# Graph-weighted attention: the next batch's graph products in one block, and the denominators moved by a burst

## The chip, the cores and the metric

The kernel runs on one core of a Trainium2 chip. The metric is device time in microseconds (us) of one launch, as the median of several runs. The core has five engines with queues of their own: TensorE (PE) for matrix products, VectorE (DVE), ScalarE (ACT) and GpSimd (POOL) for elementwise work, and SyncE (SP), which here only starts transfers. An instruction waits in its engine's queue until what it reads is written and what it overwrites has been read; the other engines go on meanwhile.

## The reference

The input x has 16 batches of 1024 nodes with 256 channels, all float32. Layer 0 is attention whose queries come from a graph product; layer 1 is a graph convolution with two batch norms. Cut to what matters here:

```python
c_adj = mean(x, over channels)                       # one number per node
A     = abs(abs(sigmoid(c_adj[m] - c_adj[n]) - 0.5) - 0.5) * 2
Wg    = adj * A                                      # 1024 x 1024 per batch
q     = relu((x.T @ Wg) * para)                      # 256 x 1024: the graph product
k, v  = x @ kv_w
out   = softmax(q k.T * scale) v                     # 4 heads of 64 channels
x     = layernorm(x + out)
x     = layernorm(x + graph_conv(x, adj, W1, b1, ..., W2, b2, ...))
```

The change touches only how the graph product, the softmax denominators and their neighbours of layer 0 are ordered.

## The kernel before

**Attention.** The work of a batch is 32 units: 2 pairs of heads, 2 halves of the queries, 8 chunks of 128 keys. Two units make a burst, so a batch has 16 bursts; `u` counts them from 0 to 15, and the fifth is `u == 4`. For a unit, `scores` (L1043) makes q k.T with four 64x64 matmuls that run side by side into a bank pair of pool "s", and ScalarE takes the exponential into a tile `p` (four buffers). `outputs` (L1059) multiplies `p` with v into two banks `po` of pool "o" (`tile_o`, two buffers), and VectorE adds `p` into `acc` for the denominators; that addition is also the last reader of a `p` buffer. Four bursts make a group (one pair, one half). After its last unit ScalarE copies `po[0]` into `oT`, VectorE adds `po[1]`, transposes the result by squares, and SP stores it; `squares_to_rows` (L1105) loads it back as rows.

**One burst behind.** The loop at L1381 emits the scores of burst j and then the outputs of burst j - 1 (`back(j - 1)`, L1389), so that ScalarE has a burst's time for the exponentials.

**Denominators.** When both halves of a pair are done, `normalise` (L1113) sums `acc` over partitions with matmuls by ones into a bank `den` of pool "t" (`tile_t`, two buffers), ScalarE copies it to `drow`, and small transfers turn it into columns. `residual` (L1138) takes the reciprocal on VectorE and scales and adds the rows into x on GpSimd. `statistics_x1` and `finish_x1` are the layer norm; the latter runs on ScalarE and ends with a GpSimd transfer of x to memory.

**Graph product.** For the next batch, `weights_abs`, `weights_tanh` (ScalarE) and `weights_adj` (VectorE) make eight tiles `wg` of 128x1024. Then 256x1024 queries come from a scheme of Strassen's kind: seven products instead of eight, each four 128x128 by 128x512 multiplications. Its sums of x are `left_first`, `left_third` and `left_last` (L849 to L859) in a tile `S` with two places; its sums of `wg`, in place, are `right(1)` to `right(4)` (L861), four subtractions each. The products share banks:

| product | reads | bank | after it |
|---|---|---|---|
| 1 | x, wg | pga | copied by ScalarE |
| 3 | S, wg | pgd | copied by ScalarE |
| 2 | x, wg | pga, accumulated | multiplied by para, rectified |
| 6 | S, wg after right(2) | pgb | added by VectorE |
| 7 | S, wg after right(3) | pgb, accumulated | added by VectorE |
| 5 | S, wg after right(1) | pgc | added twice, then weighed and rectified |
| 4 | x, wg after right(4) | pgb, accumulated | added, weighed, rectified |

"Accumulated" means that the product adds onto the bank, so VectorE or ScalarE must have read the earlier value first. All four banks are of pool "t".

**Order around the change.** The order on TensorE, ScalarE, VectorE and SP is the program's own (`manual_schedule`, L1310); semaphores follow from the tiles. Work of other kinds is emitted after `back(j - 1)` of a burst:

- u = 0: seven of the eight key and value steps of this batch, the rest of the `wg` work (`side`), the denominators of the last pair of the batch before.
- u = 1 to 3: residual, statistics of the batch before.
- u = 4 (L1419): products 1, 2, 3 with `left_first` and `right(1)`, the eighth step (keys), `finish_x1`.
- u = 5: row gather, then `load_x(b + 2)`; u = 5, 6, 7: `right(2)`, `right(3)`, `right(4)` (`between`, L920).
- u = 8 (L1428): product 6, `begin` of batch b + 2 (channel sums, reads its x), the denominators of pair 0, products 7, 5, 4.
- u = 9 to 15: one item of the next batch's `side` per burst, residual of pair 0 at 11, `transpose_squares` at 12 and 15; row gathers at 9 and 13.

At batch 14 the diagonal and the row sums of `adj`, for layer 1, come in as well.

Of the kernel before, what the change touches and what calls it, by code (L numbers as in the profile page):

```python
# [515 lines left out]
def fast_path(  # L516
# [46 lines left out]
    def tile_t(name):  # L563
        return psum["t"].tile([P, HALF], F32, tag="t", name=name)
# [168 lines left out]
    with (  # L733
# [49 lines left out]
        def prologue(b):  # L783
# [63 lines left out]
            KC = range(NCH // 2)  # L847

            def left_first():  # L849
                s2, s4 = s["S"][:, 0], s["S"][:, 1]  # L850
                nc.vector.tensor_tensor(s2, A21, A22, ALU.add)
                nc.vector.tensor_tensor(s2, s2, A11, ALU.subtract)
                nc.vector.tensor_tensor(s4, A12, s2, ALU.subtract)

            def left_third():
                nc.vector.tensor_tensor(s["S"][:, 1], A11, A21, ALU.subtract)

            def left_last():
                nc.vector.tensor_tensor(s["S"][:, 0], A21, A22, ALU.add)  # L859

            def right(k):  # L861
                for i in KC:
                    dst, one, two = {
                        1: (lo(i, H1), lo(i, H1), lo(i, H0)),
                        2: (hi(i, H1), hi(i, H1), lo(i, H1)),
                        3: (lo(i, H0), hi(i, H1), lo(i, H0)),
                        4: (hi(i, H0), hi(i, H0), hi(i, H1)),
                    }[k]
                    nc.vector.tensor_tensor(dst, one, two, ALU.subtract)
# [18 lines left out]
            def q_at(c, hs):  # L888
                return s["qT"][:, c, hs]
# [8 lines left out]

            pg = {}

            def p1():
                s["qT"] = qkv.tile([P, CC, N], F32, tag="qT", name=f"qT_{b}")
                s["S"] = xsp.tile([P, 2, NCH // 2, P], F32, tag="xS", name=f"S_{b}")
                pg["a"] = tile_t(f"pga_{b}")
                product(1, pg["a"], True)
                nc.scalar.copy(q_at(1, H0), pg["a"])  # L906
                left_first()
                right(1)

            def p3():  # L910
                pg["d"] = tile_t(f"pgd_{b}")
                product(3, pg["d"], True)
                nc.scalar.copy(q_at(0, H1), pg["d"])

            def p2():
                product(2, pg["a"], False)
                nc.vector.tensor_mul(q_at(0, H0), pg["a"], para_s[:, 0, H0])
                rectify(0, H0)

            def between(u):  # L920
                right(u - 3)
                if u == 6:
                    nc.vector.tensor_add(q_at(0, H1), q_at(0, H1), q_at(1, H0))
                if u == 7:
                    left_third()

            def p6():
                pg["b"] = tile_t(f"pgb_{b}")
                product(6, pg["b"], True)
                nc.vector.tensor_add(q_at(0, H1), pg["b"], q_at(0, H1))  # L930
                left_last()

            def p7():
                product(7, pg["b"], False)
                nc.vector.tensor_add(q_at(1, H1), pg["b"], q_at(1, H0))

            def p5():
# [7 lines left out]
            def p4():  # L945
# [81 lines left out]
            if b:  # L1027
                s["graph"] = dict(
                    between=between, p=(None, p1, p2, p3, p4, p5, p6, p7),
                )  # L1030
            return first, steps, side

# [277 lines left out]
        with tc.manual_schedule(  # L1310
# [70 lines left out]
            for j in range(len(bursts)):  # L1381
                b, u = j // PERB, j % PERB
                for i in bursts[j]:
                    scores(i)
                if u == 0:
                    steps, side = next_steps, next_side
                    next_first, next_steps, next_side = [], [], []
                if j:
                    back(j - 1)  # L1389
                if u in (5, 9, 13):  # L1390
                    run(rows_of, 1)
                if u == 5 and b + 2 < B:
                    load_x(b + 2)
                    next_first, next_steps, next_side = prologue(b + 2)
                if b == B - 1:
                    if u == 0:
                        run(sums, 1)
                        run(rows_of, 1)
                    elif u in (2, 13):
                        run(full, 2)  # L1400
                    elif u == 8:
                        run(sums, 1)
                    elif u == 3:
                        late.clear()
                elif u == 0:
                    for i in range(7):
                        if b:
                            run(steps, 1)
                            run(side, (2, 3, 2, 3, 2, 2, 99)[i])
                        if i == 1:  # L1410
                            run(sums, 1)
                            run(rows_of, 1)
                elif u < 4:
                    if u == 1:
                        run(full, 2)
                    else:
                        run(late, 1)
                    run(side, 99)
                elif u == 4:  # L1419
                    p = st[b + 1]["graph"]["p"]  # L1420
                    keys_last = steps[:1] if b else []
                    del steps[: len(keys_last)]
                    p[1]()
                    run(keys_last, 1)
                    run(late, 2)
                    p[2]()
                    p[3]()
                elif u == 8:  # L1428
                    p = st[b + 1]["graph"]["p"]
                    p[6]()  # L1430
                    run(next_first, 1)
                    run(sums, 1)
                    if b == B - 2:
                        adjacency_diagonal()
                        for n in range(6):
                            adjacency_rows(n)
                    p[7]()
                    p[5]()
                    p[4]()
                elif u < 8:  # L1440
                    st[b + 1]["graph"]["between"](u)
                else:
                    if u == 9 and b + 2 < B:
                        load_squares(b + 2, 0)
                    if u == 11:
                        run(full, 2)
# [602 lines left out]
```

## Time and profile before

| | us |
|---|---|
| median of 3 runs (2445.45 to 2446.09) | 2445.65 |
| the profiled execution's own time | 2446.41 |
| span of that execution, first to last instruction | 2444.6 |
| TensorE busy in the span | 2411.5 |
| VectorE busy | 1862.8 |
| ScalarE busy | 1238.3 |
| GpSimd busy | 475.7 |
| matmuls of scores L1051, outputs L1072 | 488.1, 485.3 |

The mean granted TensorE clock is 0.997 of full speed. Attention takes about the first 1560 us. In the profile a row names engine, line, operation and tiles (`po<-p,v`: po is written from p and v), with the count of instructions merged into it; in brackets stand idle time ahead of it and what ended that. Each 128x512 multiplication in float32 counts as two MATMUL rows. Ends of matmuls are modelled and overlap with the next, so that spacing is read from start to start.

### The profile page before, as it was taken

How to read it: one execution, taken by the hardware profiler on the slowest of the kernel's cores; microseconds unless marked ns; L12 is line 12 of the kernel's file. 1: busy time of each engine (PE TensorE's matmuls, PEld its weight loads, DVE VectorE, ACT ScalarE, POOL GpSimd, SP SyncE). 2: the span in 40 equal slices, each digit the busy share in tenths (PEclk: the TensorE clock that was granted, in tenths of full speed). 3: DMA queues.
4: the chain of work that ended last, by engine and by line, in shares of the span. 5: the costliest groups of instructions: out<-in, count | busy, mean ns of one | idle time of the engine just before them, and what ended most of it. 6: DMA issues, size and time to landing. Idle time of an engine off the chain costs nothing.

```text
span 2444.6 us, 32834 instructions
## 1 busy us (share of the span) xinstructions
PE 2411.5 (99%) x12422; PEld 1029.6 (42%) x12422; DVE 1862.8 (76%) x2570; ACT 1238.3 (51%) x1545; POOL 475.7 (19%) x486
## 2 busy tenths in 40 slices
PE   9999999999999999999999999999999999999997
PEld 5343443443434434434334343344444444444455
DVE  5688878878888888788788888956566566478978
ACT  7376675765765756657647667421110111045568
POOL 0021122111311211122112112422122122010026
PEclk9999999999999999999999999999999999999999
DMA  5124232332232332322322327221222222165559
GB/s 164 40 42 85 57 49 70 70 53 68 38 83 54 48 84 56 53 70 56 63 62 44 83 49 97 82 103 70 96 92 78 94 86 86 69 241 172 172 210 343
DMA packets 423175, 221.99 MB, mean 91 GB/s; under 512 B 361568, under 2 KB 394848, under 8 KB 414560
## 3 DMA queue, kind: packets, MB, share of 16 engines
q1 hardware_dynamic: 417648, 168.94, 28.4%
q0 software_dynamic: 4832, 50.34, 4.9%
q8 instruction: 99, 1.62, 0.3%
q14 instruction: 68, 0.56, 0.1%
q10 hardware_dynamic: 528, 0.52, 0.1%
HBM read 136.06 MB, written 83.69 MB: 90 GB/s over the span
## 4 chain that ended last, share of the span: by engine, by line
PE 86%; DVE 9%; ACT 3%; DMA 1%; issue 1%; POOL 0%; POOLq 0%; DVEq 0%
PE ps L1051 18%; PE po L1072 18%; PE pgb L883 7%; PE b_agg L1556 4%; PE pga L883 4%; PE c_agg L1556 4%; PE pk L980 4%; PE b_o L1763 3%; PE pv L993 3%; PE a_agg L1556 2%; PE b_h L1588 2%; PE pgd L883 2%; PE pgc L883 2%; PE a_o L1763 2%; PE c_o L1763 2%; PE c_h L1588 2%
## 5 line engine op out<-in xcount | busy, mean ns | idle before, releaser
L1056 ACT ACTIVATE p<-ps 128x1024 f32<-128x1024 f32 x512 | 497.6, 1021 | 183.7 <-PE ps L1051 130.1
L1082 DVE TENSOR_TENSOR acc<-acc,p 128x1024 f32<-128x1024 f32 x384 | 500.1, 1302 | 54.2 <-ACT p L1056 29.3
L1051 PE MATMUL ps<-qT,kT 64*64 64x512 f32 x4096 | 488.1, 592 | 0.3 <-ACT p L1056 0.3
L1072 PE MATMUL po<-p,v 64*64 64x512 f32 x4096 | 485.3, 589 | 0.0
L1147 POOL TENSOR_TENSOR o<-o,r_all 128x512 f32<-128x512 f32 x62 | 94.8, 1538 | 1090.8 <-DVE r_all L1141 1052.5
L1072 PEld LDWEIGHTS po<-p,v 64*64 64x64 f32 x4096 | 158.2, 133 | 281.3 <-issue 274.3
L1051 PEld LDWEIGHTS ps<-qT,kT 64*64 64x64 f32 x4096 | 151.4, 133 | 286.8 <-issue 249.2
L834 DVE SCALAR_TENSOR_TENSOR wg<-wg,adj_s 128x1024 f32<-128x1024 f32 x128 | 149.4, 1217 | 16.5 <-ACT wg L830 16.5
L825 ACT ACTIVATE wg<-crow,ccol 128x1024 f32<-128x1024 f32 x128 | 146.8, 1147 | 0.5 <-DMA crow<-c 0.5
L830 ACT ACTIVATE wg<-wg 128x1024 f32<-128x1024 f32 x128 | 136.0, 1062 | 0.9
L980 PE MATMUL pk<-xT,kvw_s 128*128 128x512 f32 x256 | 121.8, 598 | 3.1 <-ACT drow L1126 3.1
L993 PE MATMUL pv<-kvw_s,xT 128*128 128x256 f32 x512 | 124.0, 385 | 0.0
L993 PEld LDWEIGHTS pv<-kvw_s,xT 128*128 128x128 f32 x512 | 94.9, 190 | 50.0 <-issue 13.4
L893 ACT ACTIVATE qT<-qT 128x512 f32<-128x512 f32 x60 | 37.3, 629 | 149.8 <-DVE qT L896 145.2
L883 PE MATMUL pgb<-wg,S 128*128 128x512 f32 x240 | 111.0, 605 | 0.0
L883 PE MATMUL pga<-wg,x 128*128 128x512 f32 x240 | 109.6, 599 | 0.7 <-ACT qT L906 0.7
L1556 PE MATMUL a_agg<-ahT,x1l 128*128 128x512 f32 x240 | 108.1, 593 | 0.7 <-ACT agg L1298 0.7
L1148 POOL TENSOR_TENSOR x<-x,o 128x512 f32<-128x512 f32 x62 | 107.8, 1748 | 2.3
L1556 PE MATMUL b_agg<-aT,x1S 128*128 128x512 f32 x240 | 107.9, 592 | 0.0
L654 ACT COPY p_agg<-a_agg 128x512 f32<-128x512 f32 x15 | 8.8, 586 | 183.3 <-PE a_agg L1556 183.3
L690 POOL TENSOR_TENSOR x1S<-x1l 128x512 f32<-128x512 f32 x15 | 19.0, 1264 | 352.3 <-PE c_agg L1556 349.0
L1080 DVE TENSOR_TENSOR acc<-p,p 128x1024 f32<-128x1024 f32 x64 | 77.4, 1209 | 7.5 <-ACT p L1056 7.5
(230 smaller groups left out, 3511.8 us busy)
## 6 DMA issues: line engine op xcount, KB each, us to landing
h<-hw POOLq DMA_DIRECT2D x16, 2048.0 KB, 6.7
hl<-h SPq DMA_DIRECT2D x32, 1024.0 KB
x<-x POOLq DMA_DIRECT2D x16, 1024.0 KB, 4.2
x1l<-x SPq DMA_DIRECT2D x16, 1024.0 KB
xf<-x SPq DMA_DIRECT2D x16, 1024.0 KB
o<-oS SPq DMA_DIRECT2D x62, 256.0 KB
o<-o SPq DMA_DIRECT2D x248, 64.0 KB
x<-in_x_dram SPq DMA_DIRECT2D x15, 1024.0 KB
```

What stands on the lines that cost most here:

```text
L825: nc.scalar.activation(w, s["crow"], AF.Abs, bias=s["ccol"][:, n : n + 1])
L830: nc.scalar.activation(w, w, AF.Tanh, scale=0.5)
L834: nc.vector.scalar_tensor_tensor(w, w, 1.0, adj_s[:, n, :], op0=ALU.subtract, op1=ALU.mult)
L883: nc.tensor.matmul(ps, left, right, start=(start and i == 0), stop=(i == NCH // 2 - 1), skip_group_check=True,)
L980: nc.tensor.matmul(ps, kvw_s[:, c, kc * P : (kc + 1) * P], s["xT"][:, c, hs], start=(c == 0), stop=(c == CC - 1),)
L993: nc.tensor.matmul(pt[:, j * C : (j + 1) * C], s["xT"][:, c, n * P : (n + 1) * P], kvw_s[:, c, C : 2 * C], start=(c == 0), stop=(c == CC - 1),
L1051: nc.tensor.matmul(ps[kh * D : (kh + 1) * D, hd * HALF : (hd + 1) * HALF], kT[r, pr, ks], qT[r, pr, qh * HALF : (qh + 1) * HALF], start=Tr ...
L1056: nc.scalar.activation(p, ps, AF.Exp)
L1072: nc.tensor.matmul(g["po"][kh][hd * D : (hd + 1) * D, :], s["v"][r, m, h * D : (h + 1) * D], p[r, hd * HALF : (hd + 1) * HALF], start=(m = ...
L1082: nc.vector.tensor_add(g["acc"], g["acc"], p)
L1556: nc.tensor.matmul(ps, left, right, start=(start and i == 0), stop=(i == NCH // 2 - 1), skip_group_check=True,)
L1763: nc.tensor.matmul(ps, left, right, start=(start and i == 0), stop=(i == 1), skip_group_check=True,)
```

## The change

The seven products stand in one block at u = 4, in the order 1, 3, 2, then 6, then 7, 5, 4. `pga` and `pgb` come from pool "o" instead of "t". `left_first` is at the end of u = 0; two of the four subtractions of `right(1)` are at u = 1 and the other two behind product 1; `right(2)` to `right(4)` are between the products. The key step stands behind product 6, `finish_x1` and the `adj` sums between product 2 and product 6, and `load_x(b + 2)` ends the block. `begin` moves to u = 5. The denominators of pair 0 move to u = 9, between that burst's scores and the outputs of the burst before (at the last batch they stay at u = 8). The residual of pair 0 moves from u = 11 to 13, the third row gather from 13 to 15, and two `weights_adj` from u = 0 to u = 11 and 13.

```diff
             def left_first():
+                s["S"] = xsp.tile([P, 2, NCH // 2, P], F32, tag="xS", name=f"S_{b}")
...
-            def right(k):
-                for i in KC:
+            def right(k, rows=KC):
+                for i in rows:
...
-            def p1():
+            def first_three():
                 s["qT"] = qkv.tile([P, CC, N], F32, tag="qT", name=f"qT_{b}")
-                s["S"] = xsp.tile([P, 2, NCH // 2, P], F32, tag="xS", name=f"S_{b}")
-                pg["a"] = tile_t(f"pga_{b}")
+                pg["a"] = tile_o(f"pga_{b}")
                 product(1, pg["a"], True)
                 nc.scalar.copy(q_at(1, H0), pg["a"])
-                left_first()
-                right(1)
-
-            def p3():
+                right(1, KC[2:])
                 pg["d"] = tile_t(f"pgd_{b}")
                 product(3, pg["d"], True)
                 nc.scalar.copy(q_at(0, H1), pg["d"])
-
-            def p2():
+                right(2)
                 product(2, pg["a"], False)
                 nc.vector.tensor_mul(q_at(0, H0), pg["a"], para_s[:, 0, H0])
                 rectify(0, H0)
 
-            def between(u):
-                right(u - 3)
-                if u == 6:
-                    nc.vector.tensor_add(q_at(0, H1), q_at(0, H1), q_at(1, H0))
-                if u == 7:
-                    left_third()
-
             def p6():
-                pg["b"] = tile_t(f"pgb_{b}")
+                left_third()
+                right(3)
+                nc.vector.tensor_add(q_at(0, H1), q_at(0, H1), q_at(1, H0))
+                pg["b"] = tile_o(f"pgb_{b}")
                 product(6, pg["b"], True)
                 nc.vector.tensor_add(q_at(0, H1), pg["b"], q_at(0, H1))
                 left_last()
-
-            def p7():
+                right(4)
+
+            def last_three():
                 product(7, pg["b"], False)
                 nc.vector.tensor_add(q_at(1, H1), pg["b"], q_at(1, H0))
...
-                    (a, 0), (t, 0), (a, 1), (t, 1), (a, 2), (t, 2), (a, 3),
-                    (t, 3), (a, 4), (t, 4), (j, 0), (a, 5), (t, 5), (j, 1),
-                    (a, 6), (j, 2), (j, 3), (t, 6), (j, 4), (a, 7), (j, 5),
-                    (t, 7), (j, 6), (j, 7),
+                    (a, 0), (t, 0), (j, 0), (a, 1), (t, 1), (j, 1), (a, 2), (t, 2),
+                    (a, 3), (t, 3), (j, 2), (a, 4), (t, 4), (a, 5), (j, 3), (t, 5),
+                    (j, 4), (a, 6), (t, 6), (j, 5), (a, 7), (t, 7), (j, 6), (j, 7),
...
+                if u == 9 and b < B - 1:
+                    run(sums, 1)
                 if j:
                     back(j - 1)
-                if u in (5, 9, 13):
+                if u in ((5, 9, 13) if b == B - 1 else (5, 9, 15)):
                     run(rows_of, 1)
-                if u == 5 and b + 2 < B:
-                    load_x(b + 2)
-                    next_first, next_steps, next_side = prologue(b + 2)
...
-                            run(side, (2, 3, 2, 3, 2, 2, 99)[i])
+                            run(side, (2, 2, 2, 2, 2, 2, 99)[i])
...
+                    st[b + 1]["graph"]["left"]()
                 elif u == 4:
                     p = st[b + 1]["graph"]["p"]
-                    keys_last = steps[:1] if b else []
-                    del steps[: len(keys_last)]
-                    p[1]()
-                    run(keys_last, 1)
+                    p[0]()
                     run(late, 2)
-                    p[2]()
-                    p[3]()
-                elif u == 8:
-                    p = st[b + 1]["graph"]["p"]
-                    p[6]()
-                    run(next_first, 1)
-                    run(sums, 1)
                     if b == B - 2:
                         adjacency_diagonal()
                         for n in range(6):
                             adjacency_rows(n)
-                    p[7]()
-                    p[5]()
-                    p[4]()
-                elif u < 8:
-                    st[b + 1]["graph"]["between"](u)
-                else:
+                    p[1]()
+                    if b:
+                        run(steps, 1)
+                    p[2]()
+                    if b + 2 < B:
+                        load_x(b + 2)
+                        next_first, next_steps, next_side = prologue(b + 2)
+                elif u < 4:
+                    if u == 1:
+                        run(full, 2)
+                        st[b + 1]["graph"]["right"](1, range(2))
+                    else:
+                        run(late, 1)
+                elif u == 5:
+                    run(next_first, 1)
+                elif u > 8:
...
-                    if u == 11:
-                        run(full, 2)
...
+                    if u == 13:
+                        run(full, 2)
...
-                    run(next_side, 1)
+                    run(next_side, 2 if u in (11, 13) else 1)
```

More of the change, by code (lines that the diff above doesn't have):

```diff
@@ L931, in p6 @@
                 left_last()
-            def p7():
+                right(4)
+            def last_three():
                 product(7, pg["b"], False)
                 nc.vector.tensor_add(q_at(1, H1), pg["b"], q_at(1, H0))
-            def p5():
                 pg["c"] = tile_t(f"pgc_{b}")
@@ L943, in p5 @@
                     weigh(c, H1)
-            def p4():
                 product(4, pg["b"], False)
@@ L1028, in prologue @@
                 s["graph"] = dict(
-                    between=between, p=(None, p1, p2, p3, p4, p5, p6, p7),
+                    left=left_first, right=right, p=(first_three, p6, last_three),
                 )
@@ L1412, in fast_path @@
                             run(rows_of, 1)
-                elif u < 4:
-                    if u == 1:
-                        run(full, 2)
-                    else:
-                        run(late, 1)
-                    run(side, 99)
+                    st[b + 1]["graph"]["left"]()
                 elif u == 4:
                     p = st[b + 1]["graph"]["p"]
-                    keys_last = steps[:1] if b else []
-                    del steps[: len(keys_last)]
-                    p[1]()
-                    run(keys_last, 1)
+                    p[0]()
                     run(late, 2)
-                    p[2]()
-                    p[3]()
-                elif u == 8:
-                    p = st[b + 1]["graph"]["p"]
-                    p[6]()
-                    run(next_first, 1)
-                    run(sums, 1)
                     if b == B - 2:
@@ L1436, in fast_path @@
                             adjacency_rows(n)
-                    p[7]()
-                    p[5]()
-                    p[4]()
-                elif u < 8:
-                    st[b + 1]["graph"]["between"](u)
-                else:
+                    p[1]()
[14 more added lines that the diff above has]
+                elif u > 8:
                     if u == 9 and b + 2 < B:
                         load_squares(b + 2, 0)
-                    if u == 11:
-                        run(full, 2)
                     if u == 12:
```

## The prediction

> **What bounds the kernel now.** I read the page, then who waited for whom on TensorE, then one batch in order of time on each engine. Batch 10 is used below (u is the burst within it, 0 to 15); its pattern repeats every 96.69 us. Page, busy time and chain that ended last:
>
> ```profile
> PE 2411.5 (99%) x12422; PEld 1029.6 (42%) x12422; DVE 1862.8 (76%) x2570; ACT 1238.3 (51%) x1545; POOL 475.7 (19%) x486
> PE 86%; DVE 9%; ACT 3%; DMA 1%; issue 1%; POOL 0%; POOLq 0%; DVEq 0%
> ```
>
> TensorE sets the time. Its waits in the attention part sum to some 4 us after the first load, the most regular 0.22 us per batch for the denominators' copy (pk behind drow). So a change can save only matmul slots or what is lost between them, and any new TensorE wait adds in full. TensorE in order of time, around the blocks at u = 4 (batch 10) and u = 8 (batch 9):
>
> ```profile
> 1043.53 1.90 PE L1051 MATMUL ps<-qT,kT 64*64 64x512 f32 x16
> 1045.24 1.90 PE L1072 MATMUL po<-p,v 64*64 64x512 f32 x16
> 1047.07 3.70 PE L883 MATMUL pga<-wg,x 128*128 128x512 f32 x8
> 1050.61 1.88 PE L980 MATMUL pk<-xT,kvw_s 128*128 128x512 f32 x4
> ...
> 974.66 1.90 PE L1072 MATMUL po<-p,v 64*64 64x512 f32 x16
> 976.49 3.70 PE L883 MATMUL pgb<-wg,S 128*128 128x512 f32 x8
> 980.12 1.07 PE L1120 MATMUL den<-acc,ones 128*32 128x512 f32 x8
> 981.11 3.70 PE L883 MATMUL pgb<-wg,S 128*128 128x512 f32 x8
> 984.65 3.60 PE L883 MATMUL pgc<-wg,S 128*128 128x512 f32 x8
> 988.08 3.60 PE L883 MATMUL pgb<-wg,x 128*128 128x512 f32 x8
> 991.61 1.95 PE L1051 MATMUL ps<-qT,kT 64*64 64x512 f32 x16
> ```
>
> Go by the starts. A burst's scores or outputs take 1.72 us, a product 3.43, a key step 1.72; two products without a change of tile shape stand 3.43 apart (984.65 to 988.08), with one 3.53 to 3.63. At u = 4 the first product follows the outputs without a wait. ScalarE and VectorE meanwhile:
>
> ```profile
> 1041.20 1.94 ACT L1056 ACTIVATE p<-ps 128x1024 f32<-128x1024 f32 x2 [1.50 <-PE ps L1051]
> 1045.18 1.02 ACT L1056 ACTIVATE p<-ps 128x1024 f32<-128x1024 f32 x1 [2.05 <-DVE acc L1082]
> 1046.51 1.02 ACT L1056 ACTIVATE p<-ps 128x1024 f32<-128x1024 f32 x1 [0.30 <-DVE acc L1082]
> 1047.43 0.58 ACT L1089 COPY oT<-po 128x512 f32<-128x512 f32 x1
> ```
> ```profile
> 1034.86 1.22 DVE L834 SCALAR_TENSOR_TENSOR wg<-wg,adj_s 128x1024 f32<-128x1024 f32 x1 [0.92 <-ACT wg L830]
> 1036.00 1.22 DVE L1080 TENSOR_TENSOR acc<-p,p 128x1024 f32<-128x1024 f32 x1
> 1037.13 0.26 DVE L1141 RECIPROCAL r_all<-dcol 128x8 f32<-128x8 f32 x2
> 1037.32 3.21 DVE L1082 TENSOR_TENSOR acc<-acc,p 128x1024 f32<-128x1024 f32 x2
> 1041.69 0.43 DVE L618 BATCH_NORM_STATS2 st_l<-x 128x6 f32<-128x256 f32 x1 [1.16 <-POOL x L1148]
> 1043.83 2.59 DVE L1082 TENSOR_TENSOR acc<-acc,p 128x1024 f32<-128x1024 f32 x2
> 1050.91 0.68 DVE L1090 TENSOR_TENSOR oT<-po,oT 128x512 f32<-128x512 f32 x1
> ```
>
> VectorE lags from u = 1 on: the exponentials of u = 4 wait for its additions to release a p buffer, and behind them in ScalarE's queue stands the copy of po, done at 1048.01, **0.94 us after** the first product began. Now nothing waits for it, as that product writes another bank.
>
> [...] that copy runs only after the second exponential. [...] `o<-o,r_all` took 1.99 us beside VectorE's additions and 1.04 after them.
>
> **The change, part by part.**
>
> *Drains.* At u = 8 the excesses are 0.11 (into the block), 0.20 and 0.13 (into and out of the denominators), 0.11, 0.10 (out) and 0.05 (scores at 991.61, outputs at 993.38: 1.77): 0.70 us. At u = 4: 0.11 + 0.11 + 0.10 + 0.05 = 0.37. One block keeps 0.37. The denominators between scores and outputs still change shape twice, which before doesn't show: at least one 0.10 and the 0.05, at most 0.60 (nearly twice the pair 0.20 + 0.13); I take that pair once, 0.33. Saved 0.70 - 0.33 = **0.37 us** per batch (0.10 to 0.55), 15 batches. The matmuls themselves are unchanged, as are the 0.22 us behind drow: ahead of that copy stand one abs and one tanh, as before.
>
> *pga and pgb take the pool of po.* It has two banks, both held by the group that ends at u = 4; the bank released first is the one read by ScalarE's copy of po[0] (L1089). So product 1 now waits for that copy. The copy can't start before the outputs drain: at batch 0, where ScalarE is idle, it ran 81.03 to 81.62 against the first product at 80.91. The floor is so 81.66 - 80.91 = **0.75 us**, every batch. With the queue of before it is 1048.01 + 0.05 - 1047.07 = 0.99.
>
> *VectorE's work ahead of u = 4.* The three sums of `left_first` (0.65 + 0.69 + 0.69, 2.0 us in sequence: 955.57 to 957.59) move to the end of u = 0, two subtractions of `right(1)` (0.6 each, from four in 2.41) to u = 1. Two `weights_adj` (1.22 each) leave u = 0, but give nothing back: VectorE idles there and its last one waits for the last tanh (0.92 us, above), which TensorE's last value step paces. So the 2.0 us fall after 1036.0. The reciprocals and GpSimd's residual, which the statistics wait for at 1041.69, come 2.0 later; VectorE itself, busy to 1040.53, comes to 1040.53 + 2.0 + 1.2 = 1043.75. Statistics start at 1043.7 to 1044.1, a shift of 2.0 to 2.4, since GpSimd's add is slower beside VectorE. Everything behind keeps it: additions, exponentials of u = 4, copy of po. I take 2.2: copy ends 1050.2, product 1 starts 1050.26 for 1047.07, **3.2 us late** (0.75 to 3.5). Queued behind product 1 is all of TensorE.
>
> *Inside the block.* From product 2's end E: VectorE does the multiply, `left_third`, four subtractions, two adds (0.6 + 0.6 + 2.41 + 0.6 + 0.6, plus 0.3 of signals) = E + 5.1, and product 7 accumulates on the bank that the last add reads. TensorE arrives after product 6 and the key step, 3.43 + 1.72 = E + 5.15: 0.05 lost. At batch 0 there is no key step: 5.1 - 3.43 = 1.7 lost. At batch 14 the eight diagonal operations stand ahead (1464.90 to 1467.53, 2.6 us): 2.6 lost. Product 5 and 4 are ready in time (`left_last` E + 5.7 before E + 8.6; `right(4)` E + 8.1 before E + 12.0).
>
> *Moved at no cost.* `load_x` now precedes u = 5's row gathers in SP's queue and waits for the x1 store: `finish_x1` stands behind the rectify on ScalarE (E = 1050.26 + 3.54 + 2 x 3.43 = 1060.7, rectified by 1062, eight activations in 4.05), ends at 1066, store 4.2 us, load some 4.6 (issued 965.79, DMA quiet after 970.5), so 1075; `begin` reads it after product 4 (E + 15.5), its adds and u = 5's addition (2.7, as after 991.5 before): 1079. If late, VectorE and then TensorE would wait. The gathers behind it are read at u = 13 only. `begin`'s 2.9 us at u = 5 delays additions that release buffers for u = 7; the subtractions that filled u = 5 to 7 are gone. Residual at u = 13 and the third gather at u = 15 feed u = 1 and later. `weights_adj` 0 and 1 at u = 11 and 13 use idle of 1.77 and 1.15 us; without that cover the copy of v, and the denominators behind it at u = 0, would be up to 0.6 late; I take 0.1.
>
> *Sum.* Batches 1 to 13: 3.2 + 0.05 + 0.1 - 0.37 = 2.98, times 13 = 38.7. Batch 0, with VectorE idle early: 0.75 + 1.7 - 0.37 - 0.68 (product 2's wait for the copy of pga, now covered by product 3) = 1.4. Batch 14: 3.2 + 2.6 + 0.1 - 0.37 = 5.5. Together +45.6. The profiled execution took 2446.41 (span 2444.6), 0.76 above the median 2445.65; against the median: **2491 us**.
>
> **Rivals.**
> *Lag absorbed:* VectorE's extra 3.2 us is swallowed before u = 4, and product 1 loses 0.75 to 1.5. For: VectorE idles 1.16 us at 1041. Against: that idle waits for GpSimd, which shifts too. 13 x (1.1 - 0.22) + 1.4 + 3.4 = +16: 2462.
> *More than one wait:* [...] the copy of v comes 0.6 late, or pga gets the other bank and waits for VectorE's add, 3.6 us later still. [...] Against: the pool gives the first released. [...] the other bank: 2540.
> *Not slower:* only drains count. It decides where they give back what product 1's wait takes: the floor of 0.75 needs a saving of 0.75 per batch, and all of u = 8's excess is 0.70. If the denominators change shape for nothing: 15 x (0.75 - 0.70) + 1 = 2447. Against: ScalarE's lag is in the trace.
>
> **Numbers.** Likeliest 0.72 (own range 2478 to 2504), lag absorbed 0.12, more waits 0.12, not slower 0.04. The range 2460 to 2516 leaves out the not slower case and the far end of the waits. Within 0.2% (4.9 us) is about what this kernel's measurement can't tell from no change: faster 0.02, same 0.03, slower 0.95.
>
> **What would show it.** TensorE's waits: pga behind the copy of po (ACT oT), 14 times near 3 us and once near 0.7; pgb behind VectorE's add once near 1.7 and once near 2.6. In time order no change of shape at u = 8, and denominators between scores and outputs at u = 9. Statistics near 2.2 us later against u = 0's end. Wrong if pga begins without a wait, if VectorE's additions at u = 2 aren't later, or if a longer wait stands elsewhere.

## The result, and the profile after

| | before | after |
|---|---|---|
| median, us | 2445.87 (4 runs) | 2560.02 (4 runs, 2559.24 to 2560.34) |
| ratio after to before | | 1.0465 [1.0447, 1.0483] |
| profiled execution, its span, us | 2446.41, 2444.6 | 2559.24, 2557.4 |
| mean granted TensorE clock | 0.997 | 0.992 |

The change makes the kernel 114 us slower; 46 us were forecast, and the time lies outside the range. The page of the kernel after, busy time, the chain that ended last, and three groups:

```profile
PE 2436.0 (95%) x12422; PEld 1029.2 (40%) x12422; DVE 1922.6 (75%) x2570; ACT 1240.5 (49%) x1545; POOL 512.2 (20%) x486
...
PE 65%; DVE 24%; ACT 6%; issue 4%; DMA 0%; SPq 0%; DVEq 0%; POOL 0%; POOLq 0%; ACTq 0%
...
L1070 DVE TENSOR_TENSOR acc<-acc,p 128x1024 f32<-128x1024 f32 x384 | 544.9, 1419 | 30.5 <-ACT p L1044 2.4
...
L884 PE MATMUL pga<-wg,x 128*128 128x512 f32 x240 | 119.6, 645 | 32.4 <-ACT oT L1077 32.4
...
L1136 POOL TENSOR_TENSOR x<-x,o 128x512 f32<-128x512 f32 x62 | 136.3, 2217 | 0.2
```

Instruction counts are those of before, yet three busy times grew: TensorE by 25 us, VectorE by 60, GpSimd by 36. So the same instructions take longer. VectorE's additions have a mean of 1419 ns, where before it was 1302; GpSimd's `x<-x,o` has 2217, before 1748; the product into pga 645, before 599. On the chain, VectorE's share rose from 9% to 24%.

TensorE's waits in the kernel after (what waited, for whom: total us, times, longest), layer 0 alone:

```profile
PE pga L884 <- ACT oT L1077: 32.4, 15, 2.5
PE ps L1039 <- ACT p L1044: 24.6, 43, 1.1
PE den L1108 <- DVE v L987: 15.1, 14, 1.1
PE pv L982 <- DVE xT L819: 11.8, 14, 0.9
PE pxT L811 <- DMA x<-in_x_dram: 5.0, 1, 5.0
PE pgb L884 <- DVE qT L922: 4.3, 2, 2.6
PE po L1060 <- DVE oT L1078: 3.1, 1, 3.1
```

The first row is the forecast wait, with the forecast releaser: 32.4 us in 15 waits. The next three, 51.5 us, stood in no sum of mine. Apart from the first load, these waits sum to 91.3 us; before it was some 4.

TensorE in order of time in the kernel after, batch 10, from the end of u = 15 through the block at u = 0 to product 1:

```profile
1086.74 0.70 PE L982 MATMUL pv<-kvw_s,xT 128*128 128x256 f32 x2
1088.29 1.56 PE L982 MATMUL pv<-kvw_s,xT 128*128 128x256 f32 x6 [0.85 <-DVE xT L819]
1089.69 1.88 PE L969 MATMUL pk<-xT,kvw_s 128*128 128x512 f32 x4
1092.65 1.06 PE L1108 MATMUL den<-acc,ones 128*32 128x512 f32 x8 [1.08 <-DVE v L987]
...
1102.46 1.95 PE L1039 MATMUL ps<-qT,kT 64*64 64x512 f32 x16
...
1109.72 2.00 PE L1039 MATMUL ps<-qT,kT 64*64 64x512 f32 x16 [0.17 <-ACT p L1044]
...
1113.89 1.09 PE L1039 MATMUL ps<-qT,kT 64*64 64x512 f32 x8 [0.45 <-ACT p L1044]
1116.11 1.09 PE L1039 MATMUL ps<-qT,kT 64*64 64x512 f32 x8 [1.12 <-ACT p L1044]
1117.02 1.90 PE L1060 MATMUL po<-p,v 64*64 64x512 f32 x16
1121.16 5.40 PE L884 MATMUL pga<-wg,x 128*128 128x512 f32 x8 [2.25 <-ACT oT L1077]
1126.39 3.60 PE L884 MATMUL pgd<-wg,S 128*128 128x512 f32 x8
```

The reader can account for a batch by starts. Before, product 1 to product 1 took 96.69 us, of which the block at u = 0 13.93 (1019.24 to 1033.17) and from its end to product 1 13.90 (to 1047.07). After, the preceding product 1 stands at 1017.97, so the batch takes 103.19: the block at u = 0 15.72 (1086.74 to 1102.46), from its end to product 1 18.70 (to 1121.16), the rest 68.77 for 68.86. So 1.79 us are lost at u = 0 and 4.80 on the way to product 1. Of these 4.80 about 2.5 are lost ahead of and between the scores of u = 2 to 4, and 2.3 ahead of product 1 itself (4.14 us after the outputs, where 1.83 was usual). In addition this product 1 lasts 5.23 us up to the next start, where 3.54 was usual.

The windows of that stretch (window, us, TensorE busy and instructions, granted clock, DMA share, GB/s) show why:

```profile
1121.00:1122.00 1.00, 0.84 (x2) 1.00 0.00 0
...
1123.00:1124.00 1.00, 1.00 (x2) 0.50 0.00 0
...
1125.00:1126.00 1.00, 1.00 (x3) 0.61 0.00 0
```

TensorE runs at a granted clock of 0.50 for 3.41 us, behind an idle stretch of 2.25; this product 1 so takes 1.69 us more. The attention part has eight such stretches: six behind product 1, and two behind the single waits of 2.6 us (pgb at batch 14) and 3.1 (po at batch 15). Before had none there, and one in layer 1 that has gone. Seven more at 1.7 us make 12 us.

VectorE in the kernel after, around the same two places:

```profile
1078.61 8.47 DVE L1070 TENSOR_TENSOR acc<-acc,p 128x1024 f32<-128x1024 f32 x4
1087.01 1.23 DVE L819 STREAM_TRANSPOSE xT<-xS 128x1024 f32<-128x1024 f32 x1
...
1091.94 0.65 DVE L987 COPY v<-pv 128x512 f32<-128x512 f32 x1
...
1108.65 2.09 DVE L870 TENSOR_TENSOR wg<-wg 128x512 f32<-128x512 f32 x2
1110.66 4.27 DVE L1070 TENSOR_TENSOR acc<-acc,p 128x1024 f32<-128x1024 f32 x2
1114.86 0.41 DVE L618 BATCH_NORM_STATS2 st_l<-x 128x6 f32<-128x256 f32 x1
```

And GpSimd in the kernel after, the residual of pair 0 at u = 13 and that of pair 1 at u = 1:

```profile
1077.62 3.95 POOL L1135 TENSOR_TENSOR o<-o,r_all 128x512 f32<-128x512 f32 x2 [42.81 <-DVE r_all L1129]
1081.54 4.46 POOL L1136 TENSOR_TENSOR x<-x,o 128x512 f32<-128x512 f32 x2
1108.80 2.84 POOL L1135 TENSOR_TENSOR o<-o,r_all 128x512 f32<-128x512 f32 x2 [22.80 <-DVE r_all L1129]
1111.61 4.45 POOL L1136 TENSOR_TENSOR x<-x,o 128x512 f32<-128x512 f32 x2
```

In the kernel before the same four additions at u = 13 to 15 have no GpSimd beside them, and the second half of the residual at u = 1 runs beside the statistics. Its rows on VectorE and on GpSimd:

```profile
1010.02 5.21 DVE L1082 TENSOR_TENSOR acc<-acc,p 128x1024 f32<-128x1024 f32 x4
```
```profile
1041.62 1.04 POOL L1147 TENSOR_TENSOR o<-o,r_all 128x512 f32<-128x512 f32 x1
1042.74 1.27 POOL L1148 TENSOR_TENSOR x<-x,o 128x512 f32<-128x512 f32 x1
```

Four additions alone take 5.21 us; GpSimd's four operations, with only statistics beside them, would take 2 x (1.04 + 1.27) = 4.62. Together the additions take 8.47 us, 3.26 more, and GpSimd's operations 8.41, 3.8 more. So 3.26 of GpSimd's 4.62 us were added to VectorE's time: the two engines worked largely in turn. In what way they hold each other up is not shown; the time lies within the recorded operations, and no table of waits has it. Beside the statistics GpSimd's operations cost nothing that shows: these took 0.43 and 0.39 us, and 0.42 and 0.39 with GpSimd idle. My prediction gave 1.99 and 1.04 us for such an operation beside the additions and after them, but took no sum of times from them.

### The profile page after: what moved, and what is told of

The parts are those of the page before. It is cut to its first block, busy times and chain, and to the rows that moved or that the text cites. A ratio compares the mean times of both kernels' runs of the same rounds, so it can differ in the third digit from the quotient of the medians.

```text
span 2557.4 us, 32804 instructions
## 1 busy us (share of the span) xinstructions
PE 2436.0 (95%) x12422; PEld 1029.2 (40%) x12422; DVE 1922.6 (75%) x2570; ACT 1240.5 (49%) x1545; POOL 512.2 (20%) x486
## 4 chain that ended last, share of the span: by engine, by line
PE 65%; DVE 24%; ACT 6%; issue 4%; DMA 0%; SPq 0%; DVEq 0%; POOL 0%; POOLq 0%; ACTq 0%
PE po L1060 10%; PE ps L1039 10%; DVE acc L1070 8%; PE pgb L884 6%; PE pga L884 5%; PE b_agg L1538 4%; PE c_agg L1538 4%; PE b_o L1745 3%; PE pk L969 2%; PE a_agg L1538 2%; PE b_h L1570 2%; PE pgc L884 2%; PE pgd L884 2%; PE c_o L1745 2%; PE a_o L1745 2%
## 5 line engine op out<-in xcount | busy, mean ns | idle before, releaser
L1070 DVE TENSOR_TENSOR acc<-acc,p 128x1024 f32<-128x1024 f32 x384 | 544.9, 1419 | 30.5 <-ACT p L1044 2.4
L1039 PE MATMUL ps<-qT,kT 64*64 64x512 f32 x4096 | 497.1, 595 | 24.6 <-ACT p L1044 24.6
L1060 PE MATMUL po<-p,v 64*64 64x512 f32 x4096 | 490.5, 590 | 3.1 <-DVE oT L1078 3.1
L1135 POOL TENSOR_TENSOR o<-o,r_all 128x512 f32<-128x512 f32 x62 | 105.2, 1713 | 1013.0 <-DVE r_all L1129 1013.0
L884 PE MATMUL pga<-wg,x 128*128 128x512 f32 x240 | 119.6, 645 | 32.4 <-ACT oT L1077 32.4
L982 PE MATMUL pv<-kvw_s,xT 128*128 128x256 f32 x512 | 128.2, 389 | 11.8 <-DVE xT L819 11.8
L1136 POOL TENSOR_TENSOR x<-x,o 128x512 f32<-128x512 f32 x62 | 136.3, 2217 | 0.2
L1078 DVE TENSOR_TENSOR oT<-po,oT 128x512 f32<-128x512 f32 x64 | 44.0, 688 | 66.2 <-ACT oT L1077 66.1
```

Source lines behind the costliest of these rows:

```text
L884: nc.tensor.matmul(ps, left, right, start=(start and i == 0), stop=(i == NCH // 2 - 1), skip_group_check=True,)
L982: nc.tensor.matmul(pt[:, j * C : (j + 1) * C], s["xT"][:, c, n * P : (n + 1) * P], kvw_s[:, c, C : 2 * C], start=(c == 0), stop=(c == CC - 1),
L1039: nc.tensor.matmul(ps[kh * D : (kh + 1) * D, hd * HALF : (hd + 1) * HALF], kT[r, pr, ks], qT[r, pr, qh * HALF : (qh + 1) * HALF], start=Tr ...
L1060: nc.tensor.matmul(g["po"][kh][hd * D : (hd + 1) * D, :], s["v"][r, m, h * D : (h + 1) * D], p[r, hd * HALF : (hd + 1) * HALF], start=(m = ...
L1070: nc.vector.tensor_add(g["acc"], g["acc"], p)
L1136: nc.gpsimd.tensor_tensor(xs, xs, o, ALU.add)
```

## The experiments

The theory after the traces was that four causes act in series. (1) The lag of VectorE, from the sums of `left_first` and from GpSimd's turns, which makes the scores of u = 3 and 4 wait and product 1 with them. (2) The bank taken over from po. (3) Work moved to u = 11 to 15 that GpSimd's residual meets there, so that the transposed x and the copy of v come late at u = 0. (4) Half clock behind product 1's wait. The rivals: the scores' waits come from the bank wait; only one of the two moves of (3) is the cause; half clock comes from something else than product 1's wait. The first four kernels undo one part each of the kernel after; gains are given against its 2560.02 us.

**The bank given back.**

```diff
-                pg["a"] = tile_o(f"pga_{b}")
+                pg["a"] = tile_t(f"pga_{b}")
```

> The changed kernel with one edit: pga comes from pool "t" again, pgb stays in pool "o". If product 1's wait for the copy of po is a loss of its own, it goes (2.4 us start to start in 14 batches, 0.7 at batch 0) and with it the stretches at half clock (7 more than before, 1.7 us each): about 2514 us. Rival, VectorE's lag is the bound and the bank only the first place where it shows: the 2.4 us come back at product 6, which needs right(2), and the time stays near 2545.

Measured: 2516.37 us, ratio to before 1.0283 [1.0253, 1.0313], so 44 us of the 114 back. The wait of pga is gone, and with it the six half clock stretches behind it; of the attention part's eight the one of batch 14 is left. The stretch behind po at batch 15 has gone too, while layer 1 has one of 6.8 us (2.9 lost) that the kernel after lacks. So 32.4 + 7 x 1.7 - 2.9 = 41 us are accounted for, of 42.3 between the two profiled executions. The waits of the scores (24.6), the denominators (15.1) and the values (11.8) are unchanged, to the digit.

So the scores don't wait because of the bank, and the half clock in those batches follows from product 1's wait: the waits of up to 1.12 us left in place here bring none. The rival, that the time comes back at product 6, is out.

**The three sums of `left_first` back in VectorE's idle time** within u = 0, behind its fourth value step:

```diff
-                    st[b + 1]["graph"]["left"]()
+                        if i == 3:
+                            st[b + 1]["graph"]["left"]()
```

> The changed kernel with left_first emitted after the fourth step of u = 0, where VectorE idles 3.1 us ahead of the third value step's copy, and not at the end of u = 0. If the lag at u = 1 to 4 is VectorE's added work, its 2.05 us leave the path: waits of the scores and of product 1 shrink by 2.05 us per batch, 29 us, and some half-clock stretches go: 2518 to 2531. Rival, the lag comes from VectorE and GpSimd hindering each other at u = 1 and 2: those rows last as long, and the time falls by less than 10 us.

Measured: 2535.85 us, 1.0362 [1.0332, 1.0392], 24 us back. In TensorE's waits of this kernel those of the scores have shrunk from 24.6 to 3.2 us, and that of product 1 has not moved, against the expectation that both would shrink:

```profile
PE pga L884 <- ACT oT L1077: 32.4, 15, 2.5
...
PE ps L1039 <- ACT p L1044: 3.2, 15, 0.3
```

The gain is the 2.05 us by which those sums end later than the last `weights_adj` of u = 0, 14 times: 29 us. Less was measured because half clock follows product 1 in ten batches here, for six, and three stretches more in all take 5 us back. The wait of product 1 doesn't shrink, since TensorE too now arrives 2 us earlier: from the end of the block at u = 0 to product 1 it is 16.65 us for 18.70.

**The residual of pair 0 back at u = 11**, and, apart, **the two `weights_adj` back at u = 0**:

```diff
+                    if u == 11:
+                        run(full, 2)
...
-                    if u == 13:
-                        run(full, 2)
```
```diff
-                            run(side, (2, 2, 2, 2, 2, 2, 99)[i])
+                            run(side, (2, 3, 2, 3, 2, 2, 99)[i])
...
-                    run(next_side, 2 if u in (11, 13) else 1)
+                    run(next_side, 1)
```

> The changed kernel with pair 0's residual at u = 11 again (denominators stay at u = 9). If GpSimd's four operations at u = 13 to 15 are what makes VectorE late at u = 0 (additions of 2.1 us there for 1.3), the waits for xT (0.85) and for the copy of v (1.08) go, 1.8 us in 14 batches: about 2535. If the two weights_adj at u = 11 and 13 are the cause, the time stays within 5 us of 2560.

> The changed kernel with all eight weights_adj at u = 0 again (the list and the counts of before), residual still at u = 13. If the two that moved to u = 11 and 13 (2.3 us of VectorE) cause the lateness at u = 0, its 1.8 us in 14 batches go: about 2535, with no other loss, since VectorE idles at u = 0. If GpSimd at u = 13 to 15 is the cause, the time falls by less than 8 us.

Measured: 2537.77 us, 1.0370 [1.0340, 1.0400], and 2539.06, 1.0375 [1.0345, 1.0406]: 22 and 21 us back, each most of the 14 x 1.79 = 25 lost at u = 0. In both the wait of pv is gone; that of den is gone in the first and 1.5 us in the second. At batch 10 the block at u = 0 takes 14.08 and 13.94 us, for 15.72 in the kernel after. In the first, the wait for the denominators' copy is back (0.37 us a batch); in the second, the profiled execution has a mean granted clock of 0.991 for 0.992, which by these rounded figures takes some 2.5 us back. With the residual at u = 11, VectorE's four additions and the transpose that TensorE waited for read:

```profile
1066.04 5.21 DVE L1070 TENSOR_TENSOR acc<-acc,p 128x1024 f32<-128x1024 f32 x4
1071.16 1.24 DVE L819 STREAM_TRANSPOSE xT<-xS 128x1024 f32<-128x1024 f32 x1
```

The additions take 5.21 us again, for 8.47. The rival of one cause falls, and the transpose shows why. Before it ended 2.85 us ahead of the block at u = 0 (1016.39 for 1019.24). With the residual back at u = 11 it ends 1.91 us ahead (1072.40 for 1074.31), with the `weights_adj` back at u = 0 still 0.65, and with both moved it ends 1.50 us behind the block's start (1088.24 for 1086.74). Its lead covers either load alone, and not both.

The next two do one part alone in the kernel before. **The bank alone**:

```diff
-                pg["a"] = tile_t(f"pga_{b}")
+                pg["a"] = tile_o(f"pga_{b}")
```

> The kernel before with one edit: pga comes from pool "o". The bank alone makes product 1 wait for ScalarE's copy of po, which in the trace of before ends 0.99 us after that product begins (0.75 at batch 0): 14 x 0.99 + 0.75 = 14.6, so about 2460 us, with no stretch at half clock. Rival: if the copy can be overtaken or the bank of po[1] is handed out, 2446 or about 2510.

Measured: 2462.01 us beside 2446.08, 1.0063 [1.0043, 1.0083], +16. TensorE and its waits:

```profile
1055.43 1.90 PE L1072 MATMUL po<-p,v 64*64 64x512 f32 x16
1058.26 1.98 PE L883 MATMUL pga<-wg,x 128*128 128x512 f32 x4 [0.93 <-ACT oT L1089]
```
```profile
PE pga L883 <- ACT oT L1089: 14.0, 15, 1.2
```

Product 1 starts 2.83 us after the outputs, where 1.83 was usual: 1.00 lost, for a forecast of 0.99 from ScalarE's queue. The first bank that was released is the one handed out. The attention part has no stretch at half clock.

**The sums alone**: `left_first` at the end of u = 0 and two subtractions at u = 1, all else as before.

```diff
+                    st[b + 1]["graph"]["left"]()
...
+                        st[b + 1]["graph"]["right"](1, range(2))
```

> The kernel before with left_first at the end of u = 0 and two subtractions of right(1) at u = 1, as in the changed kernel, all else as it was, pga in pool "t". If VectorE's 3.2 us ahead of u = 4 delay the release of p buffers, the scores of u = 3 and 4 wait as in the changed kernel (1.7 us by its waits, 2.4 start to start): about 2479. Rival, lateness at u = 4 hurts only through the bank: 2446 to 2450.

Measured: 2482.01 us, 1.0145 [1.0124, 1.0165], +36. The scores' waits are those of the kernel after:

```profile
PE ps L1050 <- ACT p L1055: 24.6, 43, 1.1
```

So this move alone produces them. The two parts alone cost 16 + 36 = 52; together, product 1's wait more than doubles, 32.4 us for 14.0. Two runs tell what that rise doesn't need: it stays at 32.4 with `left_first` in idle time (above), and at 25.7 without GpSimd's residual (next). Common to both are the two subtractions at u = 1; no run has them alone with the bank, so their share is not shown.

**GpSimd silent.** The kernel after without GpSimd's two operations per residual; it leaves out that attention is added to x. Everything else runs.

```diff
-                nc.gpsimd.tensor_tensor(oh, oh, r, ALU.mult)
-                nc.gpsimd.tensor_tensor(xs, xs, o, ALU.add)
```

> The changed kernel without GpSimd's two operations of the residual (the attention is not added to x, for all pairs but the last of the last batch), reciprocals and transfers kept. If VectorE's and GpSimd's operations with two inputs run one after the other, the additions last 1.3 instead of 2.1 us; the waits for xT and v at u = 0 go (1.8 us), statistics start 2.4 us earlier and so does product 1: 4.2 us in 14 batches and less half clock, 2493 to 2502. If GpSimd matters only as a producer of x, which VectorE never waits for here, the time stays within 8 us of 2560.

Measured: 2491.98 us, 1.0185 [1.0165, 1.0206], 1 us below the expected range: 68 of the 114 us depend on those two lines, though GpSimd is busy for 20% of the span and no wait of TensorE names it. VectorE's additions and TensorE's waits in this kernel:

```profile
L1070 DVE TENSOR_TENSOR acc<-acc,p 128x1024 f32<-128x1024 f32 x384 | 468.1, 1219 | 31.1 <-ACT p L1044 3.0
```
```profile
PE pga L884 <- ACT oT L1077: 25.7, 15, 2.1
...
PE ps L1039 <- ACT p L1044: 2.6, 15, 0.3
```

The additions have 1219 ns each for 1419: 384 x 0.2 = 77 us less. The waits at u = 0 are gone and those of the scores nearly so, while product 1's wait, the bank's own, stays with 25.7. One half clock stretch is left behind product 1, whose wait is 2.08 us there. This run took away GpSimd's work as well as its place in the order, so 68 us is what its meeting with VectorE costs here, half clock included, not what another placing could win over the kernel before.

**What the one block is worth.** The last three keep the block, the denominators at u = 9 and the residual at u = 13. They undo what the runs above found to cost time: pga is in pool "t" again, `left_first` in idle time, all `weights_adj` at u = 0, all of `right(1)` behind product 1. At batch 14 the `adj` sums go behind the whole block (in the code `p[0]` emits products 1, 3 and 2, `p[1]` product 6, `p[2]` products 7, 5 and 4).

```diff
-                pg["a"] = tile_o(f"pga_{b}")
+                pg["a"] = tile_t(f"pga_{b}")
...
-                right(1, KC[2:])
+                right(1)
...
+                        if i == 3:
+                            st[b + 1]["graph"]["left"]()
...
                     p[2]()
+                    if b == B - 2:
+                        adjacency_diagonal()
```

> The changed kernel with pga in pool "t", left_first in VectorE's idle time in the middle of u = 0, right(1) whole behind product 1, all weights_adj at u = 0, and the diagonal and row sums of adj behind the block at batch 14. One block and the moved denominators stay. If the waits found are all that the change costs, what is left is the saved change of tile shape, 0.41 us in 15 batches, less product 7's wait at batch 0 (1.8) and 0.2 elsewhere per batch: 2441 to 2446. Rival, one block has a cost of its own (VectorE's sums can't keep up inside it): above 2455.

Measured: 2459.82 us, 1.0056 [1.0039, 1.0073], 14 above the expected range and in that of the rival, a cost of one block itself. But the regular waits are gone, and a period is 96.60 us for 96.69. The miss lies in single places: at batch 14 the row sums of `adj`, which I had put where ScalarE takes the exponentials (5.7 us), with them one half clock stretch of 6.8 us, in which TensorE stood still for the first half (1.6 us lost), and single waits of 2.1, 1.8 and 1.0 us elsewhere.

```profile
PE ps L1040 <- ACT p L1045: 6.0, 2, 5.7
```

The next version puts those sums ahead of product 7, moves `left_third` and one addition ahead of the multiply that follows product 2 so that product 7 isn't late, and keeps the row gathers and the residual of batch 14 at u = 13 and 11:

```diff
                 right(2)
+                left_third()
+                nc.vector.tensor_add(q_at(0, H1), q_at(0, H1), q_at(1, H0))
                 product(2, pg["a"], False)
...
-                    if u == 13:
+                    if u == (13 if b < B - 2 else 11):
                         run(full, 2)
```

> The merged kernel with left_third and the addition of the two copies ahead of product 2's multiply, the adj sums of batch 14 ahead of product 7, and batch 14's residual and third gather at u = 11 and 13 as before. In the merged kernel a batch takes 96.60 us from product 1 to product 1 for 96.69 before, with 0.2 us lost ahead of product 7; the rest of its 14 us are single waits at batches 0 (1.8), 14 and 15 (5.7, 2.1, 1.0) and 3.4 us of half-clock loss. Without them: 15 x 0.3 saved less 1.0 at batch 0, 2442 to 2444 us, so that one block is worth some 0.1 to 0.15% at most. Rival, something else in one block costs the 14 us: 2455 or more.

Measured: 2446.50 us beside 2446.76, ratio 0.9998 [0.9989, 1.0006]; not to be told from before, and 2.5 us above the expected range. The rival's 2455 is out. TensorE's block of batch 10:

```profile
1044.27 3.70 PE L884 MATMUL pga<-wg,x 128*128 128x512 f32 x8
...
1058.11 1.88 PE L969 MATMUL pk<-xT,kvw_s 128*128 128x512 f32 x4
1059.82 2.74 PE L884 MATMUL pgb<-wg,S 128*128 128x512 f32 x6
```

Product 7 follows the key step 1.71 us on, no longer late. The next product 1 stands at 1140.57, so a batch takes 96.30 us: 0.39 less than before, for 0.37 forecast as the saving of fewer changes of tile shape. Over 14 batches that should be 5.5 us; single waits give part of it back:

```profile
PE po L1061 <- DVE oT L1079: 2.6, 2, 2.5
```

Others are 1.1 us (den) and 0.8 (pgb at batch 0). The longest is at batch 14, where VectorE idles for a transfer of `adj` for layer 1:

```profile
1485.81 1.25 DVE L1228 STREAM_TRANSPOSE ahT<-aS 128x1024 f32<-128x1024 f32 x1 [5.19 <-DMA aS<-in_adj_dram]
```

The last one takes batch 14's denominators back to u = 8, to get that transfer away earlier:

```diff
-                if u == 9 and b < B - 1:
+                if u == 9 and b < B - 2:
                     run(sums, 1)
...
+                elif u == 8 and b == B - 2:
+                    run(sums, 1)
```

> The refined merged kernel with batch 14's denominators at the end of u = 8 again, so that the squares of adj behind them in SP's queue are loaded earlier; in the refined kernel VectorE waits 5.2 us for them and TensorE then 2.5. If that wait is what hid the saving of one block (0.39 us per batch from product 1 to product 1), the time falls by 2.5 to 3: 2443.5, a ratio of 0.9985 to 0.9990. Rival, the saving is no more than the measurement can tell: ratio 0.9993 to 1.0005.

Measured: 2446.07 us beside 2446.49, 0.9996 [0.9987, 1.0004], as the rival has it. The po wait of 2.5 us stayed, so the denominators didn't hold up that transfer. Product 1 of batch 14 stands at 1429.53, 4.3 us ahead of before's 1433.84, and layer 1's first product at 1561.86, 0.3 behind before's 1561.55: the whole saving is lost in the last two batches. The po wait is 2.5 of those 4.6 us, and behind it, a single matmul takes 1.05 us at 1490.37 and 0.59 again at 1493.77: 3.40 us as at half clock, some 1.7 lost, an estimate from the stretches above. What loses the other 0.4 was not found.

## Why the prediction was wrong in size

The terms, against the profiled execution of before (2446.41; the profiled one after has +112.8):

| term | forecast | measured | difference in all |
|---|---|---|---|
| product 1 late, batches 1 to 14 | 3.2 | 4.80 | 14 x 1.60 = 22 |
| "Moved at no cost" | 0.1 | 1.79 | 14 x 1.69 = 24 |
| half clock | none in the likeliest case | 7 x 1.7 | 12 |
| rest of the batch: saving and product 7 | -0.32 | -0.09 | 14 x 0.23 = 3 |
| batch 15: outputs wait for VectorE | 0 | 3.1 | 3 |

With the forecast 45.6 this comes to 110; some 3 us aren't placed.

**"Moved at no cost" is the step that failed most.** It looked at the two `weights_adj` against VectorE's idle time at u = 11 and 13 and found it enough; of the residual moved to u = 13 it asked only who reads the result. Each move alone fits, which the runs that put back the other show. But together with the `weights_adj` at u = 13 the residual makes VectorE's additions at u = 13 to 15 3.26 us longer, and right behind those stands the transpose that the first value step of u = 0 waits for. Its lead of 2.85 us turned into 1.50 us of lateness. The bound given there (0.6 at most, for the copy of v) left out the transpose altogether.

**The term "3.2 us late" was mis-sized; its mechanism held.** The wait is on the forecast bank, with the forecast releaser, 14 times and once at batch 0; the bank alone costs 1.00 for 0.99. The shift of VectorE was put at 2.2: 2.0 for `left_first`, which the trace has (2.04), and 0.2 for GpSimd. Measured at the statistics, from the end of the block at u = 0, it is 12.40 (1114.86 less 1102.46) for 8.52 before: 3.88. Before, only half of GpSimd's residual met two-input work, and the rest ran beside the statistics. Moved back by two us, VectorE brings two subtractions and two additions to all four: 2.01 and 4.27 us for 1.2 and 3.2. I had counted the additions as I found them, as if the overlap came along free. (The 1043.75 of that passage should read 1043.73.)

Nor did I carry the lag to TensorE before product 1. The exponentials of u = 3 and 4 are late and hold their score banks; I let TensorE arrive on time and put the whole lag on product 1, where half of it is spent earlier. That alone would not change the sum.

**Half clock** had no term in the likeliest case; what the author held of it then was an estimate that no trace had shown. In the kernel after, product 1's idle stretch of 2.25 us was followed by it in six of 14 batches, and none of the waits up to 1.12 us was; the last section tells the cases apart. The trace of before held a sign of it: in layer 1, at 2356.46, 3.41 us at a granted clock of 0.50 begin behind an idle stretch of 2.98 us, though the mean clock of that execution is 0.997. The rival "more than one wait" came nearest in kind, with the copy of v late (1.1 us for its 0.6), but not in size.

**Right**: direction and first wait; the floor of 0.75, met to the digit at batch 0 (2.58 us from the outputs to product 1, for 1.83) and more than fewer changes of tile shape save; that saving (0.39 for 0.37, seen where nothing else disturbs); product 7's wait for VectorE's addition at batches 0 and 14 (1.8 and 2.6 for 1.7 and 2.6); the denominators between scores and outputs (0.29 for 0.33); x loaded in time. Product 7 is 0.20 late (1136.69 to 1138.61, 1.92 for 1.72) for 0.05; by the prediction's own sums, ready at E + 5.1 and reached at E + 5.15, nothing was to be lost there, so its 0.05 doesn't follow.

The range failed with the terms: its upper end of 2516 was one added wait above the likeliest, and here two terms and half clock came together.

## What to carry to other kernels

Where operations with two inputs on GpSimd and VectorE come to stand side by side, the sum of their times is a first estimate (here 3.26 of 4.62 us came on top); an operation moved on either may leave a place where it was free (here beside the statistics, 0.43 and 0.39 us), or push the other's work into one where it isn't. Work that "fits into idle time" has to be summed over everything moved there, and set against the lead of the last result in that queue that another engine waits for. A bank taken from a pool whose release stands in a lagging queue turns lag that cost nothing into idle time of the engine that sets the end, here, with the bank alone, 1.00 us ahead of the longest block of the batch.

## What the runs showed of the hardware

- Two-input operations on VectorE and GpSimd ran largely in turn: four additions took 5.21 us alone and 8.47 beside four GpSimd operations; these took 1.04 and 1.27 beside the statistics and about 2.0 and 2.25 beside the additions. Statistics beside them were not slowed (0.43 and 0.39 us, for 0.42 and 0.39 with GpSimd idle).
- Half clock came in stretches of 3.41 us at a granted clock of 0.50, single or two in a row away from the kernels' ends, and cost some 1.7 us each where TensorE had work (product 1 took 5.23 us for 3.54). In the kernel after they begin at 289.51, 497.73, 705.94, 914.15, 1122.37 and 1330.58 behind product 1, 208.2 us apart, which could be the spacing of two batches; but it is also 61 times 3.413 us, and the single ones at 1555.86 and 1603.64 follow 66 and 14 times 3.413 us later. In nine of the twelve kernels, read in windows of 2 us, half clock comes more than once, and all its beginnings lie a whole number of 3.413 us apart, to within 0.1 us.
- The traces of before and after show which gaps counted there, if steps of 3.413 us are laid over TensorE's rows (with their modelled ends, and without the start and the end of the kernel). At full clock, each of the nine steps with 2.05 us or more of idle time was followed by half clock, and none with 1.92 or less. Product 1's gap of batch 10 in the kernel after has 2.2 us of idle in one step (1118.96 to 1122.37), and half clock followed; that of batch 9 is cut at 1016.55 into 0.8 and 1.4, and none followed. With GpSimd silent one of product 1's 14 gaps was followed by it, one of 2.08 us. This was read from the traces afterwards; no run was made to test it.
